# Last stage of a two-layer convolution kernel: weights loaded in pieces, buffers in three pools, normalization and PSUM tiles rearranged

## The chip, the core and the metric

The kernel runs on one core of a Trainium2 chip. The metric is the device time of one execution in microseconds (us). TensorE (PE, with its weight loads shown as PEld), VectorE (DVE), ScalarE (ACT) and GpSimd (POOL) compute; SyncE (SP), ACT and POOL also issue DMA transfers, each on a queue of its own, and 16 DMA engines carry them out. Each engine works through its instructions in order and waits on semaphores.

## What is computed

The input x is 512 x 512 x 64, float32. Two layers are added to it. Only the second, and the end of the first, matter here:

```python
x = x + _L0_conv_ref(_gn(x), ...)   # gated triangle product, ends in an output gate
x = x + _L1_conv_ref(_gn(x), w_real, w_imag)

def _L1_conv_ref(x, w_real, w_imag):
    x_ft = jnp.fft.fft2(xc, axes=(-2, -1))[:, :, :12, :12]
    out_ft = jnp.einsum('bcmn,comn->bomn', x_ft, w_real + 1j * w_imag)
    # zero padded to 512 x 512, inverse FFT, real part
```

`_gn` subtracts a mean and divides by a deviation, both over all rows and columns and one of 32 groups of 2 channels. So the second layer needs sums over the whole output of the first layer before it can add anything to any element. Since it keeps only 12 x 12 modes, the normalization can be applied to the modes: a factor for each channel, and the mean taken off mode (0, 0).

## The kernel before

The first layer is done for the 512 x 512 pairs after a compaction by a mask. Its last loop (from `for s in range(-LEAD, ...)`) goes over 8 + 32 units of 8 steps; `v` counts the 32 units of it that write output tiles of 128 x 64 x 64 elements, `n` the steps of a unit, and `last` is 31. The order in which instructions are issued in it is written by hand. In a unit, PE makes products (`w_ps`, `c_ps`, L979), DVE scales them (L1195, L1201), ACT takes a sigmoid (L1146), POOL multiplies and adds (L1038, L1042); SP stores the result in two halves (L1058) to a DRAM tensor `x1_h`. Beside that, for the second layer, DVE takes statistics of the finished tiles (L1097, 32 groups a unit) and PE sums rows into modes (`transform`, `f_ps`, L1069). For every 64 columns, `save` writes these to `modes_d` in DRAM (L1077, L1091), and `fetch` reads a quarter of the columns back (L904), from which `columns` makes the second transform (L896). In the last units:

- SP loads the mixing weights `w_real` and `w_imag`, 2304 KB each, into `wide` (L1231, at v = 30, n = 3). `wide` lies over `places(3)`, `places(4)` and the start of `places(5)`, output tiles that are used up by then.
- ACT writes the modes of the last columns but 32 (L1091), prepares a table `spread_e` (L912), and issues `fetch(3)` (L904, at v = 31, n = 4).
- PE runs `columns(3)` (L896) behind the products of the last unit, then the `transform` of the last unit, and, after a copy on ACT (L1077), the modes of the last 32 columns straight from SBUF (L1083).
- DVE finishes the statistics and joins them (L1102 to L1115, with a square and a copy on ACT, L1108 and L1109).

Then comes the tail. POOL gathers finished tiles of 1 MB (`fetch_rows`, L629), the first 15 of 64 (`AHEAD`) ahead: four of them during the last units, then five into tiles `lx_t` of a new pool, four into `place(0)` and `place(1)`, two into the space of `spread_e`. The new pools `lq` and `lx` lie over the loop's pools in SBUF. `group_norm_affine` (from L241) makes the mean (L251 to L255), the variance (L257 to L265), a reciprocal root by nine short DVE steps (L199 to L209), and factor and offset for each channel (L270 to L277). It calls `turn_sums` after the variance product, which adds the sums of modes (L1255) and turns them (L1256). DVE forms `v_modes` (L1263, L1264) and writes them, scaled, into the zeroed `picks` (L1267, L1273). PE mixes (`mixed_ps`, L1282, 36 products). `back_columns` makes a quarter of the inverse transform over columns: products `q_ps` (L1309), copies to `q_sb` on DVE (L1320) and ACT (L1322), transposes `it_ps` (L1327), copies (L1330, L1332).

The last stage takes the 64 tiles in order: four products `l_ps` (L1348), four additions on DVE (L1355), a store on SP (L1356), and the gather of the tile 15 further on, into the same buffer, once that store has landed. Three more `back_columns` come in between.

Of the kernel before, what the change touches and what calls it, by code (L numbers as in the profile page):

```python
# [19 lines left out]
C = 64  # L20
# [26 lines left out]
def conv_preact_kernel(ctx: ExitStack, tc: tile.TileContext, t: dict):  # L47
# [193 lines left out]
    def group_norm_affine(keep, sets, each, name, between=lambda: None):  # L241


        groups, n = sets[0].shape[1:]
        avg = avg_p if groups == G else avg_c
        ab = keep.tile([P, 3], F32, name="ab_" + name)
        with tc.tile_pool(name="gn_" + name, bufs=1) as gp, tc.tile_pool(
            name="gnp_" + name, bufs=1, space=PSUM
        ) as gps:
            part = gp.tile([P, groups], F32, name="part")  # L250
            nc.vector.tensor_reduce(part, sets[0], AX.X, ALU.add)  # L251
            mean_ps = gps.tile([P, groups], F32, name="mean_ps")
            nc.tensor.matmul(mean_ps, avg, part, start=True, stop=True)
# [24 lines left out]
        return ab  # L278
# [334 lines left out]
    def compact(fc):  # L613
# [193 lines left out]
        with tc.tile_pool(name="tri", bufs=1) as trp:  # L807
# [57 lines left out]
            with tc.manual_schedule(), tc.tile_pool(name="late", bufs=1) as lp:  # L865
# [65 lines left out]
                with tc.tile_pool(name="np_x", bufs=LEAD + 2) as tp, tc.tile_pool(  # L931
# [189 lines left out]
                    for s in range(-LEAD, total_g + 2 * SIZE):  # L1121
# [103 lines left out]
                        if (v, n) == (last, 4):  # L1225
                            fetch(3)
                        if (v, n) == (last, 7):
                            ends.append(columns(3, ps_t))
                        if v == last - 1 and n == 3:
                            for part, name in enumerate(("w_real", "w_imag")):  # L1230
                                nc.sync.dma_start(wide[part * C : (part + 1) * C], t[name].rearrange("c o m n -> c o (m n)"))  # L1231

                with tc.tile_pool(name="lq", bufs=1) as qp, tc.tile_pool(name="lx", bufs=1) as xp:
# [16 lines left out]
                    with tc.tile_pool(name="sps", bufs=1, space=PSUM) as sps:  # L1250
# [10 lines left out]
                        ab2 = group_norm_affine(lp, sets, 8, "x1c", turn_sums)  # L1261
                        v = qp.tile([P, 2, MODES, MODES], F32, name="v_modes")
                        nc.vector.tensor_add(v[:, 0], sums[:, :, :MODES], turned[:, :, MODES:])  # L1263
                        nc.vector.tensor_sub(v[:, 1], turned[:, :, :MODES], sums[:, :, MODES:])  # L1264
                        for k in range(2):
                            for q in range(3):
                                nc.vector.tensor_scalar(  # L1267
                                    picks[:, :, q, 12 * k + 4 * q : 12 * k + 4 * q + 4], v[:, k, :, 4 * q : 4 * q + 4],
                                    ab2[:, 0:1], None, ALU.mult,
                                )  # L1270
                            h = slice(k * C, (k + 1) * C)
                            one = picks[h, 0, 0, 12 * k : 12 * k + 1]
                            nc.vector.scalar_tensor_tensor(one, ab2[h, 1:2], float(N * N), one, ALU.mult, ALU.add)  # L1273
# [4 lines left out]
                        for m3 in range(3):  # L1278
                            for q in range(3):
                                for g in range(4):  # L1280
                                    m = MODES // 4 * g + m3
                                    nc.tensor.matmul(  # L1282
                                        mixed_ps[32 * g : 32 * g + 32, m3].rearrange("p (o g) r -> p o g r", g=4),
                                        picks[:, m, q, :], by_mode[:, :, :, m * MODES + 4 * q : m * MODES + 4 * q + 4],
                                        start=(q == 0), stop=(q == 2), tile_position=(0, 32 * g),
                                    )
                        own = picks.rearrange("p m q k -> p (m q k)")[:, : 3 * C * 4].rearrange("p (c r) -> p c r", r=4)
# [12 lines left out]
                    def back_columns(jb, pq, pt, first):  # L1300

                        it = parts[:, jb // 2, : 256 * 16].rearrange("p (j o) -> p j o", o=16)
                        for g2 in range(2):
                            ps = pq.tile([P, 2, 4, 2, C], F32, name="q_ps")[:, :, :3]
                            for part in range(2):
                                for i in range(2):
                                    g = 2 * g2 + i
                                    h = slice(32 * g, 32 * g + M2)
                                    nc.tensor.matmul(  # L1309
                                        ps[:, i, :, part, :], col_inv[h, part, jb, :], mixed[h],  # L1310
                                        start=True, stop=True, tile_position=(32 * g, 0),
                                    )
                            for i in range(2):
                                g = 2 * g2 + i
                                src = ps[:, i].rearrange("p m k o -> p (m k) o")
# [17 lines left out]
                    with tc.tile_pool(name="lpq0", bufs=2, space=PSUM) as pq, tc.tile_pool(  # L1333
# [3 lines left out]
                    with tc.tile_pool(name="lpq", bufs=1, space=PSUM) as pq, tc.tile_pool(  # L1337
# [104 lines left out]
```

## Time and profile before

| | us |
|---|---|
| median of 3 runs (lowest, highest) | 1835.98 (1834.19, 1836.71) |
| the profiled execution | 1839.54 |
| its span, first to last instruction | 1837.7 |
| busy: PE, DVE, ACT, POOL | 1637.7, 1423.6, 961.9, 945.3 |
| start of the last unit's last product on PE (L979) | 1487.91 |
| start of the first product of the last stage (L1348) | 1545.32 |
| first store of the last stage issued (L1356) | 1549.93 |
| HBM read, written over the span | 278.05 MB, 187.56 MB |

Times within the execution count from the start of the span. A line of the timeline gives the start, the duration of the instructions in it, engine and line, and in brackets how long the engine had been idle and what released it. A row of the windows gives the busy time of each engine in a stretch with the number of instructions, then the granted clock of PE as a share of full speed, the mean busy share of the 16 DMA engines, and what they moved in GB/s. The chain is followed back from the last instruction: at each step to what released it.

### The profile page before, as it was taken

To read this page: it belongs to the slowest core of one execution; us is meant where nothing else is said; L and a number is where in the kernel's file an instruction comes from. 1 tells how busy PE (TensorE), PEld (TensorE's weight loads), DVE (VectorE), ACT (ScalarE), POOL (GpSimd) and SP (SyncE) were. 2 spreads that over 40 slices of the span, in tenths; PEclk is the share of its full clock that TensorE was granted. 3 is DMA by queue.
4 is the path that set the end of the run, shared out by engine and by line. 5 is a ranking of instruction groups with operands and counts; after the bars stand their busy time and mean duration, and the time that the engine had idled before them with its cause. 6 is when DMAs were issued, how large, how long until landed. Compare 5 with 4: busy or idle time off the path is not lost.

```text
span 1837.7 us, 33577 instructions
## 1 busy us (share of the span) xinstructions
PE 1637.7 (89%) x11414; PEld 1287.7 (70%) x11414; DVE 1423.6 (77%) x2973; ACT 961.9 (52%) x1708; POOL 945.3 (51%) x711
## 2 busy tenths in 40 slices
PE   6779799999799999999999999999999866998772
PEld 5667666665678878897788888888888744665441
DVE  5989777777455547788999999999999975675552
ACT  3555555555222259976777777777777631111000
POOL 3666211111000006788999999999999862211110
PEclk9989899999899999999999999999999966555555
DMA  6999255556656513667777876776777698999999
GB/s 255 381 375 371 106 127 138 138 138 154 208 174 182 177 41 141 224 234 257 254 244 249 279 269 233 241 274 234 253 258 258 210 273 338 411 426 426 427 427 379
DMA packets 188453, 467.94 MB, mean 255 GB/s; under 512 B 34672, under 2 KB 134000, under 8 KB 147184
## 3 DMA queue, kind: packets, MB, share of 16 engines
q1 hardware_dynamic: 157376, 262.21, 42.5%
q0 software_dynamic: 27712, 201.40, 29.1%
q10 hardware_dynamic: 3184, 2.08, 0.4%
q8 instruction: 93, 1.52, 0.3%
q14 instruction: 88, 0.72, 0.1%
HBM read 278.05 MB, written 187.56 MB: 253 GB/s over the span
## 4 chain that ended last, share of the span: by engine, by line
PE 29%; DVE 16%; DMA 9%; POOL 4%; issue 3%; ACT 1%; DVEq 0%; POOLq 0%; ACTq 0%
PE c_ps L979 6%; PE w_ps L979 6%; PE t_ps L969 5%; PE l_ps L1348 4%; DVE stats2c L1097 4%; DMA places<-x_h,dst_i 4%; PE y_ps L990 4%; DVE z_t L1195 3%; DVE scratch L1012 3%; DVE z_t L1201 3%; PE f_ps L1069 2%; POOL z_t L1038 2%; DMA out_x<-places 2%; POOL places L1042 2%; DMA lx_t<-x_h,dst_i 2%
## 5 line engine op out<-in xcount | busy, mean ns | idle before, releaser
L979 PE MATMUL w_ps<-gate_x,xt_c 128*128 128x128 f32 x2048 | 280.1, 280 | 32.1 <-DVE z_t L1195 26.7
L1042 POOL TENSOR_TENSOR places<-places,z_t 128x1024 f32<-128x1024 f32 x127 | 301.2, 2371 | 8.0
L979 PEld LDWEIGHTS w_ps<-gate_x,xt_c 128*128 128x128 f32 x2048 | 251.5, 194 | 47.8 <-DVE z_t L1195 43.4
L979 PE MATMUL c_ps<-center_x,xt_c 128*128 128x128 f32 x2048 | 276.2, 278 | 1.2 <-ACT xt_c L1008 0.6
L979 PEld LDWEIGHTS c_ps<-center_x,xt_c 128*128 128x128 f32 x2048 | 252.1, 194 | 3.9 <-ACT xt_c L974 2.3
L1348 PE MATMUL l_ps<-places,rinv 24*128 24x512 f32 x512 | 207.8, 1124 | 29.3 <-DVE places L1355 18.6
L1097 DVE BATCH_NORM_STATS2 stats2c<-places 128x6 f32<-128x128 f32 x1024 | 220.5, 278 | 12.5 <-POOL places L1042 12.5
L1012 DVE TENSOR_REDUCE scratch<-sq_c 128x16 f32<-128x1024 f32 x160 | 194.6, 1216 | 27.9 <-ACT sq_c L1007 18.7
L1146 ACT ACTIVATE z_t<-z_t 128x1024 f32<-128x1024 f32 x128 | 135.5, 1059 | 133.7 <-DVE z_t L1201 116.0
L1199 POOL TENSOR_TENSOR z_t<-z_t,bias_row_out 128x1024 f32<-128x1024 f32 x32 | 75.7, 2365 | 246.6 <-DVE z_t L1195 242.5
L969 PE MATMUL t_ps<-c_ident,places 128*128 128x128 f32 x1280 | 199.0, 278 | 1.3 <-DVE places L854 1.3
L1348 PEld LDWEIGHTS l_ps<-places,rinv 24*128 24x128 f32 x512 | 120.3, 303 | 111.9 <-DVE places L1355 59.6
L969 PEld LDWEIGHTS t_ps<-c_ident,places 128*128 128x128 f32 x1280 | 144.5, 142 | 60.6 <-issue 50.3
L974 ACT ACTIVATE xt_c<-t_ps,ab_xc 128x512 f32<-128x512 f32 x256 | 176.0, 687 | 10.7 <-PE t_ps L969 9.8
L1195 DVE TENSOR_TENSOR z_t<-w_ps,rs_n 128x512 f32<-128x512 f32 x256 | 171.9, 672 | 3.7 <-PE w_ps L979 3.5
L1004 ACT ACTIVATE sq_c<-c_ps 128x512 f32<-128x512 f32 x256 | 150.5, 588 | 30.9 <-PE c_ps L979 29.4
L679 DVE BATCH_NORM_STATS2 stats1c<-x_ps 128x6 f32<-128x512 f32 x256 | 155.6, 681 | 12.5 <-PE x_ps L678 12.2
L1201 DVE TENSOR_TENSOR z_t<-z_t,scratch 128x1024 f32<-128x1024 f32 x128 | 156.3, 1221 | 10.0 <-ACT rs_n L1018 3.8
L1038 POOL TENSOR_TENSOR z_t<-z_t,places 128x1024 f32<-128x1024 f32 x64 | 151.6, 2369 | 16.2 <-ACT z_t L1146 13.3
L1355 DVE TENSOR_TENSOR places<-places,l_ps 128x512 f32<-128x512 f32 x176 | 110.2, 683 | 56.1 <-DMA places<-x_h,dst_i 45.5
L1038 POOL TENSOR_TENSOR z_t<-z_t,bias_row_out 128x1024 f32<-128x1024 f32 x63 | 149.4, 2371 | 4.6 <-ACT z_t L1146 4.0
L733 POOL COPY rbc<-rq_out 128x512 f32<-128x512 f32 x64 | 38.3, 613 | 210.0 <-DVE rq_out L209 132.0
(212 smaller groups left out, 2748.8 us busy)
## 6 DMA issues: line engine op xcount, KB each, us to landing
x_h<-places SPq DMA_DIRECT2D x64, 1024.0 KB
out_x<-places SPq DMA_DIRECT2D x44, 1024.0 KB
places<-u_d SPq DMA_DIRECT2D x512, 64.0 KB
out_x<-lx_t SPq DMA_DIRECT2D x20, 1024.0 KB
left_d<-o_c SPq DMA_DIRECT2D x64, 256.0 KB
right_d<-o_c SPq DMA_DIRECT2D x64, 256.0 KB
left_raw<-left_d SPq DMA_DIRECT2D x64, 256.0 KB
right_raw<-right_d SPq DMA_DIRECT2D x64, 256.0 KB
```

The costliest lines, as they stand in the source:

```text
L679: nc.vector.bn_stats(stats[:, 0, 16 * (jc % quarter) + 4 * r + c, :], ps.rearrange("p i k -> p (i k)"))
L969: nc.tensor.transpose(tps[:, i, :], flat[:, o : o + P], ident)
L974: nc.scalar.activation(xts[s], tps, AF.Identity, bias=ab1[:, 2:3])
L979: nc.tensor.matmul(ps[:, 2 * i : 2 * i + 2, :], xts[s][:, i, :], w, start=True, stop=True)
L1004: nc.scalar.activation(sq, cps, AF.Square)
L1012: nc.vector.tensor_reduce(totals[k % 2][:, 8 * (n - 1) : 8 * (n + 1)], sqs.pop(s // 2), AX.X, ALU.add)
L1038: nc.gpsimd.tensor_mul(zs[k, c], zs[k, c], u)
L1042: nc.gpsimd.tensor_add(xr, xr, zs.pop((k, c)))
L1097: nc.vector.bn_stats(st[k // 4][:, g, k % 4, :], x_of(k)[:, :, 2 * g : 2 * g + 2])
L1195: nc.vector.tensor_mul(z[:, 8 * odd : 8 * odd + 8, :], wps, rs)
L1201: nc.vector.tensor_add(z, z, bias_ps["ogate"].unsqueeze(1).to_broadcast([P, 16, C]))
L1348: nc.tensor.matmul(ps.rearrange("p j o -> p (j o)"), rinv[h, b, :], it[h], start=True, stop=True, tile_position=(32 * g, 0),)
```

## The change

It touches the end of the first layer's loop and the tail.

1. The weights are loaded in 8 + 8 pieces of 288 KB, a pair at each step from v = 30, n = 3 to v = 31, n = 2. `fetch(3)` is called at n = 2 in place of n = 4.
2. The five `lx_t` tiles are in three pools of 2, 2 and 1, and the list of buffers runs: first pool, second pool, `place(0)`, third pool, `place(1)`. `picks` is zeroed after four of the gathers, not ahead of them.
3. In `group_norm_affine` the sums of modes are added and turned after the product of the mean; the mean of a channel, `v_modes` and the correction of mode (0, 0) come ahead of the reciprocal root. `picks` has rows of 3 x 36 in place of 3 x 32, so that two instructions, not six, scale the modes into it.
4. `q_ps` tiles are halved to one PSUM bank each (with twice the buffers), and in the first `back_columns` DVE copies one of each pair and ACT the other.

```diff
-    def group_norm_affine(keep, sets, each, name, between=lambda: None):
+    def group_norm_affine(keep, sets, each, name, with_mean=lambda: None, with_variance=lambda ab: None):
...
             nc.tensor.matmul(mean_ps, avg, part, start=True, stop=True)
+            with_mean()
...
             nc.tensor.matmul(var_ps, avg, v, start=True, stop=True)
-            between()
+            if groups == G:
+                mine = gp.tile([P, 2, G], F32, name="mine")
+                nc.vector.scalar_tensor_tensor(mine[:, 1, :], mean, -1.0, pick, ALU.mult, ALU.mult)
+                nc.vector.tensor_reduce(ab[:, 2:3], mine[:, 1, :], AX.X, ALU.add)
+            else:
+                nc.vector.tensor_scalar(ab[:, 2:3], mean, -1.0, None, ALU.mult)
+            with_variance(ab)
             rs = rsqrt(gp, var_ps, 1.0 / n, EPS, [P, groups])
             if groups == G:
-                mine = gp.tile([P, 2, G], F32, name="mine")
                 nc.vector.tensor_mul(mine[:, 0, :], rs, pick)
-                nc.vector.tensor_mul(mine[:, 1, :], mean, pick)
-                am = gp.tile([P, 2], F32, name="am")
-                nc.vector.tensor_reduce(am, mine, AX.X, ALU.add)
-                rs, mean = am[:, 0:1], am[:, 1:2]
-            nc.vector.scalar_tensor_tensor(ab[:, 1:2], mean, -1.0, rs, ALU.mult, ALU.mult)
-            nc.vector.tensor_copy(ab[:, 0:1], rs)
-            nc.vector.tensor_scalar(ab[:, 2:3], mean, -1.0, None, ALU.mult)
+                nc.vector.tensor_reduce(ab[:, 0:1], mine[:, 0, :], AX.X, ALU.add)
+            else:
+                nc.vector.tensor_copy(ab[:, 0:1], rs)
+            nc.vector.tensor_mul(ab[:, 1:2], ab[:, 2:3], ab[:, 0:1])
...
-                        if (v, n) == (last, 4):
+                        if (v, n) == (last, 2):
                             fetch(3)
...
-                        if v == last - 1 and n == 3:
+                        i = s - (first + last - 1) * SIZE - 3
+                        if 0 <= i < 8:
+                            o = slice(i * C // 8, (i + 1) * C // 8)
                             for part, name in enumerate(("w_real", "w_imag")):
-                                nc.sync.dma_start(wide[part * C : (part + 1) * C], t[name].rearrange("c o m n -> c o (m n)"))
+                                nc.sync.dma_start(
+                                    wide[part * C : (part + 1) * C, o], t[name][:, o].rearrange("c o m n -> c o (m n)")
+                                )
...
-                    picks = qp.tile([P, MODES, 3, 32], F32, name="picks")
-                    fetch_rows(len(fetched))
-                    nc.gpsimd.memset(picks, 0.0)
-                    buffers += [xp.tile([P, JC, C], F32, name=f"lx_t{i}") for i in range(5)]
-                    buffers += [place(i)[:, r * JC : (r + 1) * JC] for i in (0, 1) for r in range(2)]
+                    picks = qp.tile([P, MODES, 3 * 36], F32, name="picks")
+                    for i, xp in enumerate(xps):
+                        buffers += [xp.tile([P, JC, C], F32, name=f"lx_t{i}_{j}") for j in range((2, 2, 1)[i])]
+                        if i > 0:
+                            buffers += [place(i - 1)[:, r * JC : (r + 1) * JC] for r in range(2)]
...
                     for i in range(len(fetched), AHEAD):
+                        if i == 8:
+                            nc.gpsimd.memset(picks, 0.0)
                         fetch_rows(i)
...
-                        ab2 = group_norm_affine(lp, sets, 8, "x1c", turn_sums)
                         v = qp.tile([P, 2, MODES, MODES], F32, name="v_modes")
-                        nc.vector.tensor_add(v[:, 0], sums[:, :, :MODES], turned[:, :, MODES:])
-                        nc.vector.tensor_sub(v[:, 1], turned[:, :, :MODES], sums[:, :, MODES:])
+
+                        def join_modes(ab):
+                            nc.vector.tensor_add(v[:, 0], sums[:, :, :MODES], turned[:, :, MODES:])
+                            nc.vector.tensor_sub(v[:, 1], turned[:, :, :MODES], sums[:, :, MODES:])
+                            for k in range(2):
+                                h = slice(k * C, (k + 1) * C)
+                                one = v[h, k, 0, 0:1]
+                                nc.vector.scalar_tensor_tensor(one, ab[h, 2:3], float(N * N), one, ALU.mult, ALU.add)
+
+                        ab2 = group_norm_affine(lp, sets, 8, "x1c", turn_sums, join_modes)
                         for k in range(2):
-                            for q in range(3):
-                                nc.vector.tensor_scalar(
-                                    picks[:, :, q, 12 * k + 4 * q : 12 * k + 4 * q + 4], v[:, k, :, 4 * q : 4 * q + 4],
-                                    ab2[:, 0:1], None, ALU.mult,
-                                )
-                            h = slice(k * C, (k + 1) * C)
-                            one = picks[h, 0, 0, 12 * k : 12 * k + 1]
-                            nc.vector.scalar_tensor_tensor(one, ab2[h, 1:2], float(N * N), one, ALU.mult, ALU.add)
+                            nc.vector.tensor_scalar(
+                                picks.rearrange("p m (q f) -> p m q f", q=3)[:, :, :, 12 * k : 12 * k + 4],
+                                v[:, k].rearrange("p m (q j) -> p m q j", q=3), ab2[:, 0:1], None, ALU.mult,
+                            )
...
-                            ps = pq.tile([P, 2, 4, 2, C], F32, name="q_ps")[:, :, :3]
+                            pair = [pq.tile([P, 4, 2, C], F32, name="q_ps")[:, :3] for _ in range(2)]
...
-                                    if first and k == 0:
+                                    if first and i == 0:
                                         nc.vector.tensor_copy(dst, src[:, :, o : o + C // 2])
...
-                    with tc.tile_pool(name="lpq0", bufs=2, space=PSUM) as pq, tc.tile_pool(
+                    with tc.tile_pool(name="lpq0", bufs=4, space=PSUM) as pq, tc.tile_pool(
...
-                    with tc.tile_pool(name="lpq", bufs=1, space=PSUM) as pq, tc.tile_pool(
+                    with tc.tile_pool(name="lpq", bufs=2, space=PSUM) as pq, tc.tile_pool(
```

More of the change, by code (lines that the diff above doesn't have):

```diff
@@ L1228, in compact @@
                             ends.append(columns(3, ps_t))
-                        if v == last - 1 and n == 3:
+                        i = s - (first + last - 1) * SIZE - 3
+                        if 0 <= i < 8:
+                            o = slice(i * C // 8, (i + 1) * C // 8)
                             for part, name in enumerate(("w_real", "w_imag")):
-                                nc.sync.dma_start(wide[part * C : (part + 1) * C], t[name].rearrange("c o m n -> c o (m n)"))
-                with tc.tile_pool(name="lq", bufs=1) as qp, tc.tile_pool(name="lx", bufs=1) as xp:
-                    picks = qp.tile([P, MODES, 3, 32], F32, name="picks")
-                    fetch_rows(len(fetched))
-                    nc.gpsimd.memset(picks, 0.0)
-                    buffers += [xp.tile([P, JC, C], F32, name=f"lx_t{i}") for i in range(5)]
-                    buffers += [place(i)[:, r * JC : (r + 1) * JC] for i in (0, 1) for r in range(2)]
+                                nc.sync.dma_start(
+                                    wide[part * C : (part + 1) * C, o], t[name][:, o].rearrange("c o m n -> c o (m n)")
+                                )
+                with tc.tile_pool(name="lq", bufs=1) as qp, tc.tile_pool(name="lx0", bufs=1) as xp0, tc.tile_pool(
+                    name="lx1", bufs=1
+                ) as xp1, tc.tile_pool(name="lx2", bufs=1) as xp2:
+                    xps = (xp0, xp1, xp2)
+                    picks = qp.tile([P, MODES, 3 * 36], F32, name="picks")
[3 more added lines that the diff above has]
+                            buffers += [place(i - 1)[:, r * JC : (r + 1) * JC] for r in range(2)]
                     spare = places[:, 7 * 64 * C - 8 * 2 * MODES * M2 : 7 * 64 * C]
@@ L1283, in compact @@
                                         mixed_ps[32 * g : 32 * g + 32, m3].rearrange("p (o g) r -> p o g r", g=4),
-                                        picks[:, m, q, :], by_mode[:, :, :, m * MODES + 4 * q : m * MODES + 4 * q + 4],
+                                        picks[:, m, 32 * q : 32 * q + 32], by_mode[:, :, :, m * MODES + 4 * q : m * MODES + 4 * q + 4],
                                         start=(q == 0), stop=(q == 2), tile_position=(0, 32 * g),
                                     )
-                        own = picks.rearrange("p m q k -> p (m q k)")[:, : 3 * C * 4].rearrange("p (c r) -> p c r", r=4)
+                        own = picks.rearrange("p m k -> p (m k)")[:, : 3 * C * 4].rearrange("p (c r) -> p c r", r=4)
                         nc.vector.tensor_mul(
@@ L1309, in back_columns @@
                                     nc.tensor.matmul(
-                                        ps[:, i, :, part, :], col_inv[h, part, jb, :], mixed[h],
+                                        pair[i][:, :, part, :], col_inv[h, part, jb, :], mixed[h],
                                         start=True, stop=True, tile_position=(32 * g, 0),
@@ L1314, in back_columns @@
                                 g = 2 * g2 + i
-                                src = ps[:, i].rearrange("p m k o -> p (m k) o")
+                                src = pair[i].rearrange("p m k o -> p (m k) o")
                                 for k, q in enumerate(qs):
```

## The prediction

> **What bounds the kernel now.** I read the page's slices first. The last seven say that the end is a stage of its own.
>
> ```profile
> DMA  6999255556656513667777876776777698999999
> GB/s 255 381 375 371 106 127 138 138 138 154 208 174 182 177 41 141 224 234 257 254 244 249 279 269 233 241 274 234 253 258 258 210 273 338 411 426 426 427 427 379
> ```
>
> From slice 35 on (1562 us, at 45.9 us a slice) the DMA engines are full at 426 GB/s, while PE and DVE have idle time. A tile of 1.049 MB in or out takes 2.46 us of DMA. So nothing that computes there can be won. What can be won is the start of this stage, and DMA time lost ahead of it. Windows of 5 us show where the rate drops:
>
> ```profile
> 1505.00:1510.00 5.00, 5.00 (x25) 2.27 (x24) 1.02 (x3) 0.00 (x0) 0.00 (x0) 0.50 1.02 431
> 1510.00:1515.00 5.00, 4.24 (x20) 2.50 (x18) 1.13 (x3) 1.13 (x3) 1.57 (x2) 0.50 0.74 236
> 1515.00:1520.00 5.00, 2.83 (x20) 1.74 (x16) 1.75 (x5) 0.00 (x0) 3.78 (x5) 0.93 0.92 323
> ...
> 1540.00:1545.00 5.00, 3.65 (x16) 3.27 (x16) 2.47 (x3) 2.26 (x3) 0.00 (x0) 0.50 0.83 346
> 1545.00:1550.00 5.00, 3.92 (x14) 2.05 (x15) 2.48 (x4) 0.26 (x1) 0.00 (x0) 0.50 0.04 16
> ```
>
> At 1545 all 15 tiles ahead are in, and DMA waits 5 us for the first store (1549.93). After it 64 stores and 49 gathers are left, in the new kernel too. So the end moves with the first store, as long as the 15 tiles land ahead of it. The chain of waits says what that store hangs on:
>
> ```profile
> 1485.32 16.11 DMA places<-modes_d
> 1501.44 0.04 issue
> 1501.48 5.31 PE t_ps L896 x24
> 1506.80 3.67 PE f_ps L1069 x16
> ...
> 1511.12 6.37 PE t_ps L1083 x32
> 1517.49 0.60 PE mean_ps L253 x2
> ```
>
> `fetch(3)`, 576 KB, takes 16.11 us, and PE stands still for 11.9 of them. What it is behind are the weights, as SP's waits between 1430 and 1560 us and two windows show:
>
> ```profile
> SPq L1231 <- DMA modes_d<-places: 19.0, 1, 19.0
> ```
> ```profile
> 1462.00:1476.00 14.00, 10.09 (x64) 7.50 (x64) 13.83 (x36) 6.72 (x8) 12.87 (x7) 0.88 1.05 253
> ...
> 1500.00:1512.00 12.00, 9.76 (x44) 6.46 (x46) 6.43 (x28) 1.13 (x3) 0.00 (x0) 0.50 0.98 411
> ```
>
> While `w_real` moves (from 1461.95, 64 packets of 36,864 bytes), the engines are full at 253 GB/s only, and ACT's writes to `modes_d`, issued at 1468.4, land at 1481.5. `w_imag` waits for these (19.0 us), goes at 1481.5, and stands in front of `fetch(3)`.
>
> **The change, part by part.**
>
> *Weights in pieces, `fetch(3)` earlier.* The built program gives the semaphores. SP issues the first pair at 1462. The second waits for ACT's first write to `modes_d`; with only 0.6 MB of weights ahead of it I put this at 1472. Then come six pieces, the store of unit 30's first half, two pieces, and the sixth pair, which waits for `fetch(3)`: a new wait, with the rest of the pieces and the last three stores queued behind it on SP. ACT issues `fetch(3)` within its first 12 table steps (from 1479.97, 0.355 us each), at about 1481.4. For its landing I have two ends: 1.4 us of data after a fast start, or the 5.8 us that the page gives for a 1 MB gather; so 1484 to 1488. SP then needs 6 x 0.5 us for the other pieces, so they are in by about 1495.
>
> PE's products end at 1487.91 + 1.68 = 1489.6, so L896 starts there: 5.31 us to 1494.9. The second half of the last `transform` waits for POOL's last addition (1495.32 + 2.34 = 1497.7): half of 3.67, to 1499.5. ACT's copy 0.6, L1083 6.37: 1506.5, not 1517.5. `fetch(3)` may land as late as 1490 at no cost.
>
> Now DVE is late next: its statistics are unbroken to 1506.1. ACT's square starts at once, no longer behind the copy (in the trace at 1510.97): 0.03 + 0.56. DVE's L1114 starts at 1506.75 (before 1511.56), and the partial mean ends 1.26 later, at 1508.0, behind L1083. L253 to L255 take 0.7: the mean stands at 1508.75, before at 1518.12. **Gain 9.4.**
>
> *Sums and mean ahead of the root.* Before, 8.85 us lie between the mean and the first mixing product (1526.97). L1255 (0.45) moves under the mean's product, which covers it: 0.6 us of PE round trip. After the variance's sum (2.02, unchanged) come four steps and two small ones: two at 0.22, two at 0.22 (L1263, L1264), two at 0.1, together 1.1, where 0.5 of PE's product was waited for anyway. The root stays at 2.02. Behind it: product 0.2, sum 0.25, factor 0.1, two scalings of 144 elements at 0.3 as L1263, 0.1 to PE: 1.25. Sum 2.02 + 1.1 + 2.02 + 1.25 = 6.4, a gain of 2.4. But 1.77 of it is this:
>
> ```profile
> 1524.40 0.54 DVE L1267 TENSOR_SCALAR picks<-v_modes,ab_x1c 128x48 f32<-128x48 f32 x3
> 1526.71 0.16 DVE L1273 SCALAR_TENSOR_TENSOR picks<-ab_x1c,picks 64x1 f32<-64x1 f32 x1 [1.77 <-DVE picks L1267]
> ```
>
> The same instruction 2.4 us earlier waited for nothing. If the stall belongs to the place (code being loaded, say), it comes back somewhere and the gain is 0.7. I take the near row, the first L1273: **2.4, else 0.7.** The same function at the start of the kernel loses one step of 0.1: nothing.
>
> *PSUM tiles.* Before, DVE and ACT take turns on one tile:
>
> ```profile
> 1537.57 0.48 DVE L1320 COPY q_sb<-q_ps 128x192 f32<-128x192 f32 x1 [1.68 <-PE q_ps L1309]
> 1538.60 0.80 DVE L1320 COPY q_sb<-q_ps 128x192 f32<-128x192 f32 x2 [0.55 <-ACT q_sb L1322]
> 1539.94 0.48 DVE L1320 COPY q_sb<-q_ps 128x192 f32<-128x192 f32 x1 [0.55 <-ACT q_sb L1322]
> ```
>
> The transposes start at 1540.57, 3.0 us after the first copy. Apart, each engine makes four copies of about 0.4 without a pause, and the first transposes need three: 1.4. **Gain 1.5**, bounds 0.8 and 1.9. The three later `back_columns` lie under full DMA: nothing.
>
> *Buffers.* POOL waits 13.3 us here (until 1512.8) before it gathers into the new pool, for all that lies below it. Now the first two tiles wait for the last product (1489.6), the next two for DVE's last output step (1495.6), `place(0)` for eight statistics (1498.3), the third pool for L1115 (1507.6), the rest for stores and PE. POOL gets to them at 1498.9, and at 1.25 us each is through by 1513. By itself that gives no time; it keeps the first store from being early for nothing. DMA then has one store, 12 tiles and 0.8 MB of constants, 13.7 x 2.46 = 34 us from 1498.5: in at 1532.5.
>
> *Sum.* 9.4 + 2.4 + 1.5 = 13.3: first store at 1536.6, 4 us after the last tile. Other steps (mixing 6.96, transposes) stay. As a check by DMA time: the windows from 1510 to 1580 lack 13 us of full rate; 4 us of idle and the 4 us of starting up remain, and some 8 us of stores and gathers are done earlier, between 1475 and 1497: 13 again. The profiled execution is 3.56 us (0.2%) above the median; the gain is taken off the median: 1836.0 - 13.3 = **1822.7**.
>
> *A rule against it.* The Trainium skill, "DMA: Bandwidth & Descriptors", section "Measured (HBM→SBUF, 128 partitions, SWDGE, issued from GpSimd)", asks for transfers of at least 1 MiB, and its section "Anatomy of one DMA" puts about 2.0 us of fixed cost on each. By it, as an estimate, a piece is 2.7 us, and 16 one after the other 43 us in place of 15: 1462 to 1505, with SP's wait for `fetch(3)` to 1515, just where the mixing wants them. The row says otherwise of the large ones: 2.36 MB in 14 us, not 7.4. Size is not their limit, and up to eight pieces are in flight. I go by the row; even the rule costs nothing here.
>
> **Rivals.**
>
> *A. As summed*, 1822.7, or 1824.4 with the stall: 0.65.
>
> *B. The head start is partly eaten.* POOL now issues six or seven gathers (0.94 us each) and the zeroing while DVE still makes statistics. If each stops DVE, the 9.4 shrinks by 6 to 7: 1829. Against: an issue at 1484.82 left DVE's statistics at 0.86 for four, as elsewhere. Or the tiles land after the first store, with the same result: 0.23.
>
> *C. Nothing to be seen:* the fetch is slow for reasons of its own, 16 us again from 1481.4 to 1497.5. Then L896, transform, copy and L1083 end at 1513.5, leaving 4 of the 9.4; if the stall and the turns stay as well, 1832: 0.07.
>
> *D. Slower.* The new wait on SP decides. The mixing waits for all 16 pieces, six of these for `fetch(3)`. If they compete with the gathers from 1499 on, they land late. The point is 1526.97 + 1.5 = 1528.5: later, and each us is a loss. That asks for 33 us after `fetch(3)`'s expected landing at the latest, when 1.8 MB at half the rate is 8. A last piece at 1535 would give 1842: 0.03.
>
> *E. More:* PE's clock, 0.50 for most of the tail, comes up sooner, since PE no longer stops at 1489.6; mixing at full clock is 3 us less: 1819. 0.02 alone.
>
> **Range and chances.** A with its stall and a few us to either side, and most of B: 1819 to 1830. A measurement of this kernel tells about 0.2%, 3.7 us. Faster takes A, B, E and a third of C: 0.92. Same 0.05, slower 0.03.
>
> **What would show it.** `fetch(3)` landing by 1490 and L896 without a wait; L1083's end at 1506 to 1507 and DVE's partial mean as the later of the two; 6.4 us from mean to mixing; 1.5 us between first copy and first transpose; DMA full from 1498 to 1532, a gap of 3 to 5 us, and the first store at 1536 to 1537. Wrong, if statistics stretch beyond 1508, if the mixing waits for a DMA, or if the last stage falls below 425 GB/s.

## The result, and the profile after

The changed kernel takes 1826.96 us (median of 6 runs, 1824.57 to 1828.73), the kernel before 1834.31 us in the same comparison (6 runs, 1832.61 to 1836.71). The ratio is 0.9953, with a 95% interval of 0.9942 to 0.9965: 8.6 us less, between 6.4 and 10.6. (The ratio is that of the comparison as recorded; it is not the quotient of the two medians, which differ by 7.4 us.) Forecast were 1822.7 us with a range from 1819 to 1830. The profiled execution after took 1827.94 us with a span of 1826.1 us.

The loop ahead of the tail is the same code in both, but shifts between executions by up to some 6 us. So a place in the tail is counted here from C, the start of ACT's copy of the modes of column group 14 (L1077, after the change L1080). It comes 5.8 us behind the first issue of weights before and 5.9 us after, so it marks the same place in both loops. C is 1467.79 us before and 1471.71 us after. By the trace, the first store of the last stage is issued at C + 82.1 before and at C + 67.7 after.

The page's slices after, DMA share and rate. The 34th of the 40 is at 414 GB/s where it was at 338, and the last five are full at 426 GB/s as before, but for the very last:

```profile
DMA  6999245555655512576866776777668689999999
GB/s 253 386 385 370 102 124 137 137 138 149 203 184 175 183 58 117 197 275 237 274 238 243 258 254 229 252 268 271 241 228 291 218 251 414 423 427 426 427 427 382
```

The windows of 5 us, after (stretch, length, busy time of PE, PE's loads, DVE, ACT and POOL, PE's clock, DMA share, GB/s):

```profile
1505.00:1510.00 5.00, 5.00 (x32) 2.61 (x31) 4.91 (x23) 0.00 (x0) 4.22 (x5) 0.72 1.02 431
1510.00:1515.00 5.00, 1.48 (x8) 0.59 (x4) 3.91 (x11) 0.64 (x2) 3.31 (x4) 0.97 1.00 418
...
1535.00:1540.00 5.00, 3.54 (x16) 1.89 (x17) 3.10 (x6) 0.65 (x1) 0.00 (x0) 0.84 1.01 421
1540.00:1545.00 5.00, 5.00 (x17) 3.46 (x14) 4.49 (x8) 0.00 (x0) 0.00 (x0) 0.50 1.03 426
1545.00:1550.00 5.00, 5.00 (x21) 3.30 (x18) 4.45 (x8) 0.00 (x0) 1.44 (x2) 0.50 1.02 388
```

The hole of before (236 GB/s at 1510, 16 GB/s at 1545) is gone, and so is the gap ahead of the first store (1539.37): the row at 1535 has 421 GB/s.

PE's timeline after, with what each group waited for:

```profile
1494.36 2.76 PE L899 MATMUL t_ps<-col_basis,places 96*128 96x24 f32 x24
...
1504.82 5.58 PE L1086 MATMUL t_ps<-places 128*64 128x288 f32 x32 [0.76 <-ACT places L1080]
1512.52 0.38 PE L253 MATMUL mean_ps<-part,c_avg_p 128*128 128x32 f32 x2 [2.13 <-DVE part L251]
...
1519.13 6.92 PE L1298 MATMUL mixed_ps<-places,picks 128*32 128x256 f32 x72 [3.47 <-DVE picks L1286]
```

L899 (before: L896) starts straight behind the products, where it had waited 11.9 us for `fetch(3)`. The mean's product now waits for DVE (L251), no longer for PE's L1086 (before: L1083). From mean (1512.94 on DVE) to mixing it is 6.19 us, where it was 8.85.

### The profile page after: what moved, and what is told of

Its sections match the earlier page's. It is cut to its first block, busy times and chain, and to the rows that moved or that the text cites. A ratio compares the mean times of both kernels' runs of the same rounds, so it can differ in the third digit from the quotient of the medians.

```text
span 1826.1 us, 33612 instructions
## 1 busy us (share of the span) xinstructions
PE 1643.6 (90%) x11414; PEld 1290.0 (71%) x11414; DVE 1422.8 (78%) x2968; ACT 961.5 (53%) x1708; POOL 945.0 (52%) x711
## 5 line engine op out<-in xcount | busy, mean ns | idle before, releaser
L977 ACT ACTIVATE xt_c<-t_ps,ab_xc 128x512 f32<-128x512 f32 x256 | 176.0, 688 | 14.7 <-PE t_ps L972 13.6
L1007 ACT ACTIVATE sq_c<-c_ps 128x512 f32<-128x512 f32 x256 | 150.5, 588 | 32.8 <-PE c_ps L982 31.3
```

What stands on the lines that cost most here:

```text
L977: nc.scalar.activation(xts[s], tps, AF.Identity, bias=ab1[:, 2:3])
L1007: nc.scalar.activation(sq, cps, AF.Square)
```

## The experiments

Two theories stand behind the expectations. **S**: the end moves with the first store, so steps ahead of it count one for one. **F**: the DMA engines are full from about 1500 us on, so what they have still to move by then sets the end. **R**, used in one run, says that the weights move slowly because a transfer of them reaches only 64 partitions.

For each profiled execution the table has, counted from C, the mean, the first mixing product, the time at which the 15 tiles ahead are in (the end of the last packet of their gathers), the first store, and the end of the span. "Lost" is the DMA time lost between 1500 and 1600 us: 5 us x (1 - rate / 426 GB/s), summed over the windows of 5 us that are below 426. Column "us" has medians of all runs, those of the kernel before in the four comparisons being 1834.31, 1835.33, 1834.81 and 1834.86 us. Ratios are those of the comparisons as recorded; quotients of the medians differ from them by up to 0.0009.

A profiled execution is one of the runs, and most lie within 2.1 us of their median. The first one of before is 5.2 us above it and weights in 128 rows 5.1 us; all but weights is 4.3 us below, early weights 2.9 and 3.8 us.

| kernel | us | ratio, 95% | mean | mixing | tiles in | store | end | lost |
|---|---|---|---|---|---|---|---|---|
| before, first profile | 1834.31 | | 50.3 | 59.2 | 79.7 | 82.1 | 369.9 | 13.5 |
| before again | 1835.27 | 1.0000 (0.9987, 1.0014) | 47.2 | 54.4 | 77.6 | 77.1 | 363.1 | 8.2 |
| pools only | 1835.28 | 0.9999 (0.9989, 1.0010) | 47.7 | 55.0 | 74.9 | 76.5 | 363.6 | 8.4 |
| steps only | 1834.59 | 0.9992 (0.9982, 1.0001) | 47.4 | 53.7 | 78.6 | 75.7 | 361.9 | 6.8 |
| all but weights | 1830.93 | 0.9967 (0.9951, 0.9982) | 47.5 | 53.7 | 75.0 | 71.2 | 356.4 | 1.3 |
| weights only | 1831.26 | 0.9973 (0.9960, 0.9987) | 41.2 | 48.7 | 73.0 | 73.5 | 359.9 | 7.7 |
| weights and pools | 1831.00 | 0.9972 (0.9958, 0.9986) | 41.8 | 49.1 | 71.0 | 70.5 | 359.0 | 7.2 |
| after | 1826.96 | 0.9953 (0.9942, 0.9965) | 41.2 | 47.4 | 71.5 | 67.7 | 354.4 | 3.0 |
| after again | 1825.67 | 0.9950 (0.9935, 0.9965) | 41.2 | 47.5 | 72.8 | 66.7 | 355.0 | 1.4 |
| early weights | 1824.20 | 0.9942 (0.9923, 0.9962) | 40.8 | 47.2 | 67.6 | 64.8 | 350.9 | 3.5 |
| early weights again | 1824.44 | 0.9943 (0.9930, 0.9957) | 40.8 | 47.2 | 67.4 | 64.8 | 351.0 | 3.5 |
| weights in 128 rows | 1824.93 | 0.9939 (0.9920, 0.9955) | 41.0 | 47.6 | 67.4 | 67.8 | 355.7 | 9.0 |
| no weights | 1823.84 | 0.9935 (0.9917, 0.9953) | 40.8 | 47.0 | 67.5 | 65.1 | 352.3 | 5.8 |
| all at once | 1824.97 | 0.9938 (0.9920, 0.9955) | 41.1 | 47.3 | 75.9 | 64.8 | 355.6 | 0.5 |

The end comes 285 to 288 us behind the later of tiles and store where the tiles are the later by no more than 0.5 us, and 280 to 285 us behind it where they are later by 2.4 to 11.1 us.

### Before again

No edit.

> The kernel before, unchanged, once more: what two profiles and two sets of runs of one program differ by. In the changed kernel's profile the loop of the first layer is 4.4 us late by its last unit, in two jumps of about 2 us (near 880 us and near 1400 us). If these belong to an execution, this profile is off by jumps of that size too, somewhere, against the first profile of before; if they belong to the change, it agrees with it within 1 us. The time is the same within 0.1%.

Time: the same (ratio 1.0000). But its profile differs from the first one of the same code by 4.9 us of span and 5.0 us at the first store. PE's timeline of this execution:

```profile
1512.32 4.17 PE L1083 MATMUL t_ps<-places 128*64 128x288 f32 x32 [0.77 <-ACT places L1077]
...
1524.09 7.29 PE L1282 MATMUL mixed_ps<-places,picks 128*32 128x256 f32 x72 [3.98 <-issue]
1533.47 0.95 PE L1309 MATMUL q_ps<-mixed,col_inv 24*128 24x192 f32 x16 [2.09 <-issue]
1537.42 3.65 PE L1327 MATMUL it_ps<-c_ident,q_sb 128*128 128x128 f32 x16 [3.00 <-DVE q_sb L1320]
```

and two rows of DVE's, and the window in which L1083 lies:

```profile
1523.23 0.57 DVE L1267 TENSOR_SCALAR picks<-v_modes,ab_x1c 128x48 f32<-128x48 f32 x3
1523.83 0.16 DVE L1273 SCALAR_TENSOR_TENSOR picks<-ab_x1c,picks 64x1 f32<-64x1 f32 x1
```
```profile
1510.00:1515.00 5.00, 4.23 (x30) 2.40 (x24) 1.15 (x3) 1.14 (x3) 0.67 (x1) 0.87 0.92 332
```

L1083 took 4.17 us here, not 6.37, since PE's clock came back to full in this window (0.87 on the mean, against 0.50). The pause of 1.77 us ahead of the second L1273 isn't there. `q_ps` takes 0.95 us, not 1.59. So the first profile of before is no typical tail, and its differences belong to the execution: the mean is at C + 47.2 here, and at C + 47.4 to 47.7 in the three other runs that have the old weight loads.

### Weights only

Part 1 of the change alone, on the kernel before: the pieces and `fetch(3)` at n = 2.

> Part 1 alone on the kernel before: weights in 16 pieces and the earlier fetch. Theory F (full DMA): in the changed kernel DMA is full from about 1500 us to the end, so the end is set by what is left to move at that time, and a tail that computes faster than DMA fills the 15 tiles gains nothing. Then this part alone gives nearly all of the change: 8 us. Theory S (first store): the end moves with the first store of the last stage, and the gain came out at two thirds of the forecast for other reasons; then this part gives 9.4 of the 13.3 us, times two thirds: 6 us. In both the first store comes about 9 us earlier against the last product of the loop.

4 us less in medians, 5.0 by the ratio. The mean stands 6.0 us sooner than in the repeated profile of before, the store only 3.6. The rest went in the mixing: PE paused in it, in steps with no waiting that the trace shows,

```profile
1518.72 4.90 PE L1286 MATMUL mixed_ps<-places,picks 128*32 128x256 f32 x46 [4.25 <-DVE picks L1277]
1524.42 0.38 PE L1286 MATMUL mixed_ps<-places,picks 128*32 128x256 f32 x1 [0.80 <-issue]
1525.13 0.40 PE L1286 MATMUL mixed_ps<-places,picks 128*32 128x256 f32 x1 [0.33 <-issue]
```

so that mixing took 9.4 us here (1518.72 to 1528.09), where it is 5.5 to 7.3 us in most others. It did so in "steps only" as well (8.4 us). In both POOL issued gathers late (from 1511 and 1515 us on), but so it did in the two profiles of before, where mixing took 6.9 and 7.3 us. What PE paused for is open.

### All but weights

The changed kernel with part 1 undone.

> The changed kernel with part 1 undone: large weight loads and the late fetch again, with the three pools, the new order of the normalization and the split PSUM tiles. The chain still hangs on the fetch (16 us). First store 3.9 us earlier than before. By theory F 3.9 us faster than before, since DMA still has a gap ahead of the first store; by theory S two thirds of it, 2.6.

6.0 us less by the ratio (between 3.3 and 9.0), 4.4 by the medians, where F had asked for 3.9 and S for 2.6. The mean is where it was, so all of it lies behind the mean. Of the 5.9 us at the first store, the change's own steps are 1.0 (mean to mixing) and 1.8 (`q_ps` to transposes, 2.19 for 3.95); most of the rest is PE, whose clock was full from 1528 to 1540 us in this execution (`it_ps` to `l_ps` 3.04 us, against 4.74). How typical that is isn't known: this execution is 4.3 us faster than the median of its kernel.

### Weights and pools

Parts 1 and 2 on the kernel before.

> Parts 1 and 2 on the kernel before, without the new normalization and the split PSUM tiles. The first store comes about 4 us later than in the changed kernel. By theory F at most 2 us slower than the changed kernel, 7 to 8 us faster than before, with DMA full or nearly so from 1500 us on. By theory S all of the 4 us is lost: 4.6 us faster than before.

The same as weights only, within their intervals; nearer to the 4.6 us of S than to the 7 to 8 of F. Gathers into the new pools start 9.6 us sooner (1503.2 us, C + 31.3, not 1511.0, C + 40.9) at no gain: from 1540 to 1560 us DMA waits for the first store and loses 4.5 us (272, 362, 287 and 397 GB/s in its four windows).

### Pools only, and steps only

Pools only is part 2 on the kernel before; steps only is parts 3 and 4 on it, with the old pool and order of buffers.

> The kernel before with the buffers in three pools only. The gathers start some 13 us sooner (1500 in place of 1513), no step ahead of the first store changes. Theory S: within 1 us of before, 1835. Theory F: DMA work moves ahead of the first store, where the engines stood still for 5 us; the end comes 3 to 5 us sooner, 1831. In the weights-and-pools run the pools added nothing to the weights, but there the engines were full.

> The kernel before with the sums and mean joined ahead of the root and the PSUM tiles split only; weights and pools as before. By the prediction's terms the first store is 3.9 us earlier, 2.2 if the pause of 1.77 us was the one execution's own. Theory S: 1831 to 1833. Theory F: the gathers start late here and the DMA engines are full up to the first store, so a part of it is lost: 1833 to 1835. Together with the pools' run it splits the 6.0 us of the run of all but the weights.

Neither gives a time that can be told from before (the steps' interval reaches from 3.3 us less to no change), though both together gave 6.0 us. Added up, the two ratios make 0.9991; the 2.4 thousandths from there to 0.9967 are just clear of the noise of the three (2.1). The windows show a reason. Pools only:

```profile
1535.00:1540.00 5.00, 3.72 (x20) 3.35 (x20) 2.09 (x3) 2.55 (x3) 0.00 (x0) 0.50 1.01 421
1540.00:1545.00 5.00, 4.24 (x15) 2.37 (x16) 2.60 (x5) 0.00 (x0) 0.00 (x0) 0.50 0.25 102
1545.00:1550.00 5.00, 5.00 (x17) 3.36 (x15) 4.63 (x8) 0.00 (x0) 0.46 (x1) 0.50 0.90 364
```

Steps only:

```profile
1510.00:1515.00 5.00, 4.23 (x29) 1.78 (x23) 0.99 (x3) 1.13 (x3) 0.00 (x0) 0.78 0.95 371
1515.00:1520.00 5.00, 3.67 (x26) 2.46 (x22) 2.37 (x7) 0.00 (x0) 3.63 (x4) 1.00 0.83 249
...
1540.00:1545.00 5.00, 3.14 (x12) 1.17 (x11) 1.99 (x4) 1.01 (x1) 0.00 (x0) 0.50 1.01 419
```

All but weights:

```profile
1510.00:1515.00 5.00, 4.23 (x38) 3.18 (x32) 1.14 (x3) 1.14 (x3) 1.95 (x3) 0.99 1.01 424
1515.00:1520.00 5.00, 2.05 (x12) 0.96 (x7) 4.01 (x17) 0.00 (x0) 1.01 (x2) 1.00 1.02 421
...
1540.00:1545.00 5.00, 5.00 (x16) 3.34 (x15) 4.68 (x9) 0.00 (x0) 0.00 (x0) 0.58 1.01 423
```

With the pools alone the tiles are in early (C + 74.9) and DMA then waits for the same store (C + 76.5): 8.4 us lost, as before. With the steps alone the gathers still start late (249 GB/s at 1515) and DMA is full right up to the first store (C + 75.7), so a store that comes sooner finds tiles still moving (in at C + 78.6). Only both leave neither hole: 1.3 us lost, though in a fast execution. So the end goes, near enough, by the later of two chains, the tiles' transfers and the first store, and the kernel before had them near each other (C + 77.6 and 77.1). Theory F's 3 to 5 us for the pools fell; S's 2 to 4 us for the steps are not borne out, but their interval reaches into them.

### Four ways to load the weights

On the changed kernel, each with part 1 altered. Early weights: pairs at other steps, and the last writes to `modes_d` on SP's queue.

```diff
-                            queue = nc.scalar if jc == NJ - 2 else nc.sync
+                            queue = nc.sync
...
-                        i = s - (first + last - 1) * SIZE - 3
-                        if 0 <= i < 8:
+                        i = s - (first + last - 2) * SIZE - 3
+                        i = i if 0 <= i < 3 else i - 5 if 8 <= i < 13 else -1
+                        if i >= 0:
```

> The changed kernel with three of the eight pairs of weight pieces a unit earlier (v = 29, n = 3 to 5, when DMA has idle time), the other five at v = 30, n = 3 to 7, and the last writes of modes on SP's queue in place of ACT's, so that no piece waits for a transfer of another queue. Theory F (full DMA): the end is set by what DMA has left to move at about 1500 us; 1.8 MB of weights and up to three stores that the changed kernel moves between 1493 and 1503 are then done earlier. 2 to 4 us faster than the changed kernel, 11 us faster than before. Theory S (the first store alone): the first store stays where it is against the loop, so no difference to the changed kernel.

Weights in 128 rows, eight transfers of 576 KB, in which the weights come to lie in another order:

```diff
-                            o = slice(i * C // 8, (i + 1) * C // 8)
-                            for part, name in enumerate(("w_real", "w_imag")):
...
+                            src = t[("w_real", "w_imag")[i // 4]].rearrange("c (h o) m n -> (c h) o (m n)", h=2)
+                            nc.sync.dma_start(wide[:, 8 * i : 8 * i + 8], src[:, 8 * (i % 4) : 8 * (i % 4) + 8])
```

> The changed kernel with the same weight bytes loaded by eight transfers over all 128 partitions instead of 16 over 64 (rows of 4,608 bytes as before). The weights stand in another order in the buffer, so the mixing computes with permuted weights. It measures the rate: theory R (rows): the weights move at some 250 GB/s with full engines because a transfer reaches only half of the partitions; then they move at about 400 here, DMA has less left at 1500 us and the end comes 2 to 4 us earlier than in the changed kernel. Rival: the low rate comes from the company of small packets or from HBM; then rate and time are as in the changed kernel.

No weights leaves out these lines altogether.

> The changed kernel without the weight loads: the mixing takes what stands in the buffer. The ceiling for anything done to the weights. By theory F 4 to 6 us faster than the changed kernel, until the gathers that POOL issues from 1499 us on are the first thing DMA has to do; by theory S no more than 1 us, since in the changed kernel neither the fetch nor the mixing waits for the weights.

All at once issues the 16 pieces at v = 30, n = 3.

```diff
-                        if 0 <= i < 8:
+                        for i in range(8) if i == 0 else ():
```

> The changed kernel with all 16 pieces issued at v = 30, n = 3, ahead of the stores of unit 30. If the spacing over eight steps matters, the stores and the fetch are held up as with the two large loads, and it is 2 us or more slower than the changed kernel. If the size of the pieces is what matters, since the semaphores of earlier transfers hold them back anyway, it is the same within 1 us.

The four lie within 1.1 us of each other, and their intervals overlap those of the changed kernel. Three windows of the run in 128 rows, and then one of the changed kernel. The sizes of the packets in the trace (4,608 bytes for weights, 8,192 for stores and gathers) tell what moves: mostly weights in the first, stores and gathers in the second, stores in the third, weights alone in that of the changed kernel:

```profile
1485.00:1490.00 5.00, 4.31 (x24) 2.22 (x24) 2.80 (x8) 4.18 (x12) 4.88 (x3) 1.00 1.03 388
1495.00:1500.00 5.00, 4.69 (x33) 2.87 (x32) 4.56 (x13) 2.32 (x3) 4.92 (x3) 0.82 0.94 393
1500.00:1505.00 5.00, 1.93 (x8) 0.20 (x8) 5.00 (x21) 0.26 (x1) 4.47 (x4) 0.50 0.58 238
```
```profile
1495.00:1500.00 5.00, 4.13 (x27) 2.30 (x26) 4.57 (x13) 1.74 (x2) 4.92 (x3) 0.76 0.99 242
```

R was right about the rate: full engines move 388 GB/s of weights in place of 242. The two large loads of before had moved at 253 GB/s with full engines, so the size of a transfer is not the reason. In this execution the time won is lost again: the tiles are in at C + 67.4, 4.1 us sooner than after, but DMA has little to do at 1500 us (238 GB/s) and later waits for a first store that comes as late as after, C + 67.8; 9.0 us lost, in place of 3.0. It is an execution 5.1 us above its median, though. By the ratios 2.0 to 2.6 us were won, as R had asked, but the intervals don't tell that from nothing.

In no weights 4.7 MB less are moved, 11 us of full rate. Against the changed kernel, each beside its own before, this is 1.5 to 1.8 thousandths by the ratios, some 3 us, between what S (1) and F (4 to 6) had asked: about the most that another way of loading could give. In all at once it is the other way round: the store is issued at C + 64.8, and nothing is lost (0.5 us), but the tiles are in only at C + 75.9. Within 30 us of C, DMA has moved 7.1 MB there and 7.9 MB in the changed kernel. So the end doesn't follow the store.

That store, and that of early weights, is not early by the loading: mixing starts within 0.2 us of where it does after. PE's clock was full behind it, so that `it_ps` to `l_ps` took 3.04 us, not 4.75. The window of all at once:

```profile
1525.00:1530.00 5.00, 2.87 (x24) 2.04 (x24) 3.11 (x6) 3.14 (x6) 0.00 (x0) 1.00 1.01 419
```

### After again, and early weights again

Unaltered copies of both, on one chip.

> The changed kernel once more, on the chip of the three runs beside it. All theories: 1826.5 us, ratio 0.9955, as a base for the next run. Between executions the loop ahead of the tail shifts by some 2 us and PE's clock in the tail differs, so the profiled execution may lie 3 us to either side.

> The kernel with the early weights once more, so that the changed kernel stands beside it. In the first look its first store came 64.8 us after the last copy ahead of the weights, the changed kernel's 67.7. Theory S (the end moves with the first store): 2.5 us below the changed kernel, 1824. Theory F (the DMA engines are full from 1500 us on, and what they had to do by then sets the end): the pieces moved ahead of 1490 are DMA time gained as well, the same 2 to 3 us. Rival (the difference was an execution's own): within 1 us of the changed kernel.

1825.67 and 1824.44 us: 1.2 us apart, with intervals that overlap for the most part. Early weights has its store 1.9 us sooner and its tiles in 5.4 us sooner, but loses 2.1 us more. Counted from C, its two profiled executions end 3.4 to 4.1 us sooner than the two of the changed kernel; but both are 2.9 us or more below their medians. That it is the faster kernel isn't shown.

## Why the prediction was right, and where its sum failed

**The direction and the mechanism** held. The first store was forecast 13.3 us sooner, at C + 68.8, and came at C + 67.7. Rivals C (nothing to be seen) and D (slower) didn't come about; D's point, a mixing that waits for the pieces, had 3.47 us of waiting for DVE and none for DMA. (By D's own times its 33 us are 40, from 1488 to 1528.5; nothing hangs on it.) Of B's two forms the first, POOL's issues stopping DVE, didn't come about: the last 40 statistics took 7.82 us, and 7.80 before. The second did: the tiles landed at C + 71.5, 3.8 us after the first store. E's full clock came for L899 (2.76 us in place of 5.31) but not for the mixing, 6.92 us in both profiles. The point was 4.3 us too low. The range held because its upper part was kept for the stall and for B, not for what made the sum too large; to that extent it was luck.

**Earlier fetch, to the mean.** Forecast was a mean at 1508.75, which is C + 41.0; it came at C + 41.2. L899 had no wait; the partial mean ended at 1512.38, C + 40.7 (forecast C + 40.2), behind L1086 as forecast, whose end at C + 38.7 is the forecast one (by two errors that cancel: the `transform` ended 0.6 us later, and L1086 took 5.58 us, not 6.37). ACT issued the fetch at 1484.49, C + 12.8, where C + 13.6 was forecast, and it took 9 us, longer than either end of the estimate. That cost nothing, but only just: it was in at 1493.7, C + 22.0, and the text allowed for 1490, C + 22.2. The fixed point was right, but the gain of 9.4 was counted from a row of one execution. L1083's 6.37 us are 4.17 in the repeated profile of before, in pools only, in steps only and in all but weights, so that the mean of before stands at C + 47.2 to 47.7 there, not at C + 50.3. The term is worth 6.2 us.

**Mean to mixing.** Forecast 6.4, measured 6.19 (after) and 6.25 (after again, all but weights). Before it is 7.23 us without the pause, so the term is worth 1.0, not 2.4. The text held two values ready, 2.4 and 0.7, and chose by an argument about a place in the code; that the pause belonged to one execution wasn't among its cases. One more profile would have told.

**PSUM tiles.** The four copies follow each other without a pause, and the transposes start 1.29 us after the first (1529.66 to 1530.95), forecast 1.5:

```profile
1529.66 1.45 DVE L1336 COPY q_sb<-q_ps 128x192 f32<-128x192 f32 x4 [1.60 <-PE q_ps L1325]
```

A gain of 1.7 against 3.0 in both profiles of before. Right.

**The sum, and the step that failed.** 6.2 + 1.0 + 1.7 = 8.9, and 8.6 (6.4 to 10.6) were measured. Counted from C, the end comes 8.1 to 8.7 us sooner in the two profiles after than in the repeated one of before. The prediction's 13.3 failed in its last step, "the profiled execution is 3.56 us (0.2%) above the median; the gain is taken off the median". Of the 5 us by which that execution's tail was slow, 4.4 were counted as gains of the change (3.2 in the first term, 1.4 in the second, -0.2 in the third), and then taken off a median that doesn't hold them. Taken off the execution that they came from, it is 1839.54 - 13.3 = 1826.2, against 1827.94 for the profiled execution after; that the two agree so well is in part luck, as the loop ahead was 3.9 us later in the latter. In terms of DMA time: from one profile to the other the span falls by 11.6 us, 10.5 of it lost DMA time and 1.1 the rest; the first profile of before lay 5.2 above the median of its six runs, that after 1.0 above its own, and 11.6 - 4.2 is the 7.4 us between the medians.

**The gap of 3 to 5 us ahead of the first store** was wrong, and so was the check by DMA time behind it. "Some 8 us of stores and gathers are done earlier, between 1475 and 1497": in the first 30 us from C it is 7.9 MB after and 6.1 MB before, 4.2 us of full rate. What held them back are SP's waits, between 1430 and 1560 us after:

```profile
SPq L1236 <- DMA places<-modes_d: 12.5, 1, 12.5
SPq L1236 <- DMA modes_d<-places: 7.7, 1, 7.7
```

The first is the new wait that the prediction named. (Early weights, in which no piece waits for ACT's queue, has its tiles in at C + 67.4 to 67.6.) It lasts until 1493.7, so the last six pieces are issued from 1493.7 to 1497.6, and the last three stores of the loop from 1498.8 to 1502.4, into the time in which the gathers run. The tiles were forecast in at 1532.5 (C + 64.7), 4 us ahead of the first store, and came at C + 71.5, 3.8 us behind it. It cost little: the end is C + 354.4, and store-bound runs (pools only, weights in 128 rows), which end 287 to 288 us behind the store, would put it at C + 355 to 356. But it took away the slack, and with it what a still earlier store could bring (all at once shows that).

**Buffers.** "By itself that gives no time; it keeps the first store from being early for nothing." Both halves fit: pools only 0.9999, and the steps without the pools 0.9992 where with them 0.9967.

**The rule against it.** The Trainium skill's "DMA: Bandwidth & Descriptors" asks, in "Measured (HBM→SBUF, 128 partitions, SWDGE, issued from GpSimd)", for 1 MiB or more. Its figures are for transfers issued from GpSimd, and these pieces are issued from SP. 288 KB pieces were no loss here: 242 GB/s, and 253 for the large loads. By their packets six pieces moved in the 10 us from 1475 us, 1.7 us each, where the estimate had 2.7. What moved the rate was the number of rows (388 GB/s over 128), which that section holds fixed.

**What stays open.** Whether the two halves of the change add is not settled: weights alone 5.0 and all but weights 6.0 are 11.0 by the ratios, together 8.6; by the medians they are 4.1 and 4.4, together 7.4 and, in the second comparison, 9.2; the intervals cover both. That all but weights is already bound by full DMA (1.3 us lost) would explain a sum that falls short, but its profiled execution also had the better PE clock, and no run takes that away. What stops PE inside the mixing in two runs isn't known.

## What to carry over

Count places in a tail from a mark that the change doesn't move. Take a gain off the execution whose rows it was summed from, and look at a second profile of the same kernel before pauses of 1 to 2 us and clock-bound rows are booked as gains. Where a stage starts when the later of two chains is through, a part that shortens one of them may be worth nothing alone and some us together with the other, so cost parts in pairs. DMA time lost, summed from windows, tells the two apart: lost time means that a step is late, and none lost means that only moving bytes ahead of the stage helps.

## What the runs showed of the hardware

- PE's granted clock switches between 1.00 and 0.50 in the tail, in stretches of some 3 to 27 us up to the first store, whose places differ from execution to execution of the same code (the clock record of the two traces of before); 32 products took 4.17 us at a mean clock of 0.87 and 6.37 us at 0.50, and `it_ps` to `l_ps` 3.04 us at 1.00 and 4.74 us at about 0.5.
- Weights loaded into 64 partitions kept all 16 engines full (DMA share 0.99) at 242 GB/s, the same weights over 128 partitions (1.03) at 388 GB/s.
- A transfer's issue on SP waited 12.5 and 7.7 us for transfers of ACT's queue (after), and held everything behind it on SP.
